# A GRU gate stage by one level of Strassen's product, with PSUM split in two pools

## The chip, the cores and the metric

The kernel runs on one core of a Trainium2 chip. The metric is the device time of one execution in microseconds; lower is better. TensorE multiplies matrices into PSUM (eight banks of 128 x 512 fp32), VectorE (DVE), ScalarE (ACT) and GpSimd (POOL) work elementwise, and DMA queues (issued from SyncE, SP, and from GpSimd) move data between HBM and SBUF. All numbers are fp32. In the profile an fp32 matmul appears as two MATMUL records, each with its weight load (PEld).

## The reference, cut to what matters

The input x holds 128 graphs of 128 nodes with 256 features. Layer 0 is a normalisation and ReLU, then a gated graph network; layer 1 is five small graph convolutions over the first 25 nodes of each graph. The change is in the gates of layer 0 (h is the normalised input, d = 256):

```python
x_in = concatenate([x_conv, x_nmp], axis=-1)       # 512 features
gi = x_in @ w_ih.T + b_ih                          # 512 -> 768
gh = h @ w_hh.T + b_hh                             # 256 -> 768
r = sigmoid(gi_r + gh_r)
z = sigmoid(gi_z + gh_z)
nn_ = tanh(gi_n + r * gh_n)
out0 = (1.0 - z) * nn_ + z * h
x = x + out0
```

x_conv is a pair of one-dimensional convolutions (1 tap and 17 taps), x_nmp a dense message passing over the adjacency.

## The kernel before, in words

The 128 graphs are worked on in 32 groups q of four graphs (4 x 128 = 512 columns, features on the partitions as two chunks of 128). Each group goes through these programs, which are Python generators:

- stage_a(q), eight groups per batch: load x (tile xa), normalise it, transpose it to hT (stored to HBM as hTd), first convolution (pc), Fourier transform of its nodes (pf) into X.
- stage_b(bat), four batches: the 17-tap convolution as products per frequency (pa, pb), with weights wf loaded from HBM and summed on GpSimd (lines 474, 475) and the results y combined on VectorE (lines 503 to 505) and stored to HBM as yd.
- stage_n(q): the messages (pse, pm, pd, pt, px) into xm.
- stage_c(q): the inverse transform (pi, line 638) and its ReLU give xc; then the gates (line 656); then the output.
- prepare(blk) and block(blk): layer 1, eight blocks of 16 graphs, in the second half.

The order of instructions on every engine is fixed before the run. `Order.run` takes steps from two lanes: a step ends at a `yield cost, delay`, and the lane with the least cost done (divided by its weight) goes next. Each engine then works through its own queue strictly in that order, and waits at semaphores where it needs another engine. The groups' lane runs stage_n and stage_c with two programs in flight; the other lane first holds stage_a and stage_b, then layer 1. Stage_c of the next group may start as soon as the last gate of the group before it is issued (G_DONE), and its output waits for the group before (C_DONE).

In stage_c the inverse transform makes, for each feature half co, one PSUM tile of 128 x 512 with eight matmuls, which VectorE then reads (line 640, scale and add hT) and ScalarE finishes (line 642). A gate is one PSUM tile of 128 x 512: six weight chunks of 128 x 128 for r and z (two on hT, two on xm, two on xc), and for n four chunks on xm and xc in one tile (pn) and two on hT in another (pg). The order is, for each half dc: r, pg, n, z. ScalarE takes sigmoid and tanh out of PSUM or SBUF (lines 662, 676, 681), VectorE does two operations (lines 666, 675), GpSimd three operations of 128 x 512 (lines 684, 685, 687): d = hT - n, d = d z, go = d + n. Then po transposes go back and VectorE adds it to x (line 706).

PSUM is two pools of four banks: pacc (pa, pb, pw, pi, the gates, the large tiles of layer 1 and half of the pd tiles) and ptmp (all else).

Of the kernel before, what the change touches and what calls it, by code (L numbers as in the profile page):

```python
# [9 lines left out]
FP = mybir.dt.float32  # L10
# [7 lines left out]
HID = 512  # L18
# [189 lines left out]
def kernel(ctx: ExitStack, tc: tile.TileContext, x, adj, consts, vecs, w_se, conv1_w,  # L208
# [8 lines left out]
    pacc = ctx.enter_context(tc.tile_pool(name="pacc", bufs=4, space=PSUM))  # L217
# [94 lines left out]

    def fold_embedding():

        nc.vector.memset(wse9, 0.0)
        for role in range(3):
            nc.vector.tensor_copy(wse9[:, :, 3 * role:3 * role + 3], wse[:, :, :3])
        pbs = ptmp.tile([P, 512], FP, tag="tmp", name="pbs")
        nc.tensor.matmul(pbs[:, :1], c("sel"), v("b_se"), start=True, stop=True)
        bse = cp.tile([P, 1], FP, name="bse")  # L320
        nc.vector.tensor_copy(bse, pbs[:, :1])
        nc.vector.scalar_tensor_tensor(embb, emb[:, 4:8], bse, emb[:, 8:12],
                                       op0=ALU.mult, op1=ALU.add)
        yield 1.5, 0.0
# [15 lines left out]
    def load_xa(q):  # L340
        LOADED.add(q)
        XA[q] = ab.tile([P, 4, D], FP, tag="xa", name=f"xa{q}", bufs=3)
        load_x(XA[q], q)

    def stage_a(q):
# [3 lines left out]
        for n in range(q, min(q + 3, NQ)):  # L349
            if n not in LOADED:  # L350
                load_xa(n)
# [6 lines left out]
        hT = ab.tile([P, 2, 512], FP, tag="hTa", name=f"hTa{q}")  # L358
# [7 lines left out]
        yield 0.9, 1.5  # L366
        nc.gpsimd.dma_start(out=hTd[q], in_=hT)
        h1 = ab.tile([P, GB, D], FP, tag="h1", name=f"h1{q}")
# [32 lines left out]
    def tap_weights():  # L401
# [23 lines left out]
        for n in range(4):  # L425
            for m in range(8):
                if m % 4 == 0:
                    ws = tw.tile([P, 2, 8, D], FP, tag="ws", name=f"ws{n}_{m}")
                pws = [pacc.tile([P, 2, D], FP, tag="acc", name=f"pw{n}_{m}_{h}")
# [16 lines left out]
        LATE["wih"] = weight(wg, w_ih, [P, 4, 3 * D], "(k p) o -> p k o", "wih", nc.sync)  # L446
        LATE["whh"] = weight(wg, w_hh, [P, 2, 3 * D], "(k p) o -> p k o", "whh", nc.sync)
# [6 lines left out]
    def stage_b(bat):  # L454
# [31 lines left out]
        for f in range(NF + 1):  # L486
# [5 lines left out]
            pa = pacc.tile([P, 2, D], FP, tag="acc", name=f"pa{bat}_{f}")  # L492
            for s in range(2):
                product(pa[:, s], lambda k: X[:, k, 2 * f + s], f, s)
            if f == 0:
                nc.vector.tensor_copy(y, pa)
            else:
                pac = xf.tile([P, 2, D], FP, tag="pac", name=f"pac{bat}_{f}", bufs=2)
                nc.scalar.activation(pac, pa, AF.Copy)  # L499
                pb = pacc.tile([P, D], FP, tag="acc", name=f"pb{bat}_{f}")  # L500
                xs = XS.pop(f)
                product(pb, lambda k: xs[:, k], f, 2)
                nc.vector.tensor_sub(y[:, 0], pac[:, 0], pac[:, 1])  # L503
                nc.vector.tensor_add(pac[:, 0], pac[:, 0], pac[:, 1])
                nc.vector.tensor_sub(y[:, 1], pb, pac[:, 0])
# [18 lines left out]
    def load_c2(q):  # L524
        yt = LATE["io"].tile([HB, 2 * GB, D], FP, tag="yt", name=f"yt{q}")
        x0 = q % BQ * 2 * GB
        nc.sync.dma_start(
            out=yt, in_=yd[q // BQ].rearrange("(x b) f c -> (b f) x c", b=NB // 2)
            [:, x0:x0 + 2 * GB])
        xt = LATE["io"].tile([P, 4, D], FP, tag="xt", name=f"xt{q}")  # L530
        load_x(xt, q)
        IN2[q] = yt, xt

    def neighbours(q, hT, ad, xm):
# [20 lines left out]
        for h in range(2):  # L555
            pm = ptmp.tile([P, 2, D], FP, tag="tmp", name=f"pm{q}_{h}")
            for i in range(2):
# [10 lines left out]
        pds = [(ptmp, pacc)[i % 2].tile([P, N], FP, tag=("tmp", "acc")[i % 2], name=f"pd{q}_{i}")  # L568
               for i in range(GB)]
        pt = ptmp.tile([P, GB, N], FP, tag="tmp", name=f"pt{q}")  # L570
        aT = LATE["fr"].tile([P, GB, N], FP, tag="aT", name=f"aT{q}")
        for j in range(GB):
            rows = slice(j * WIDE, (j + 1) * WIDE)
            nc.tensor.matmul(pds[j], lr[rows, 0], lr[rows, 1], start=True, stop=True)
        for j in range(GB):
            nc.tensor.transpose(pt[:, j], ad[:, j], ident)
        for j in range(GB):
            nc.scalar.activation(aT[:, j], pds[j], AF.Exp)
        nc.vector.tensor_mul(aT, aT, pt)
# [43 lines left out]
    def stage_c(q):  # L623
# [6 lines left out]
        if q not in IN2:  # L630
            load_c2(q)
            yield 0.0, 6.0
        yt, xt = IN2.pop(q)
        xc = LATE["fr"].tile([P, 2, 512], FP, tag="xc", name=f"xc{q}")
        for co in range(2):
            pc = pacc.tile([P, 512], FP, tag="acc", name=f"pi{q}_{co}")
            for a in range(2 * GB):
                nc.tensor.matmul(pc[:, a * 64:(a + 1) * 64], yt[:, a, co * P:(co + 1) * P],  # L638
                                 inv[:HB], start=True, stop=True)
            nc.vector.scalar_tensor_tensor(xc[:, co], pc, scl["bn2"][:, co:co + 1], hT[:, co],  # L640
                                           op0=ALU.mult, op1=ALU.add)
            nc.scalar.activation(xc[:, co], xc[:, co], AF.Relu, bias=sft["bn2"][:, co:co + 1])
            yield 1.75, 0.0

        xin = [(2, xm[:, 0]), (3, xm[:, 1]), (0, xc[:, 0]), (1, xc[:, 1])]
        wih, whh = LATE["wih"], LATE["whh"]
        go = LATE["fr"].tile([P, 2, 512], FP, tag="go", name=f"go{q}")

        def gate(ps, col, ih, hh):
            ops = []  # L650
            if hh:
                ops += [(whh[:, k, col:col + P], hT[:, k]) for k in range(2)]
            if ih:
                ops += [(wih[:, i, col:col + P], a) for i, a in xin]
            for i, (w, a) in enumerate(ops):
                nc.tensor.matmul(ps, w, a, start=(i == 0), stop=(i == len(ops) - 1))  # L656

        for dc in range(2):
            pr = pacc.tile([P, 512], FP, tag="acc", name=f"pr{q}_{dc}")
            gate(pr, dc * P, True, True)  # L660
            r = LATE["fr"].tile([P, 512], FP, tag="r", name=f"r{q}_{dc}")
            nc.scalar.activation(r, pr, AF.Sigmoid, bias=brz[:, dc:dc + 1])  # L662
            yield 5.2, 0.0
            ph = pacc.tile([P, 512], FP, tag="acc", name=f"pg{q}_{dc}")
            gate(ph, 2 * D + dc * P, False, True)
            nc.vector.scalar_tensor_tensor(r, ph, v("b_hh", 4 + dc), r, op0=ALU.add, op1=ALU.mult)
            yield 1.75, 0.0
            if not dc:
                while q and q - 1 not in C_DONE:
                    yield 0.0, 0.5  # L670
                if q + 1 < NQ and (q + 1) // BQ in B_DONE:
                    load_c2(q + 1)
            pn = pacc.tile([P, 512], FP, tag="acc", name=f"pn{q}_{dc}")
            gate(pn, 2 * D + dc * P, True, False)
            nc.vector.tensor_add(r, r, pn)  # L675
            nc.scalar.activation(r, r, AF.Tanh, bias=v("b_ih", 4 + dc))  # L676
            yield 3.45, 0.0
            pz = pacc.tile([P, 512], FP, tag="acc", name=f"pz{q}_{dc}")
            gate(pz, D + dc * P, True, True)
            z = LATE["fr"].tile([P, 512], FP, tag="z", name=f"z{q}_{dc}")  # L680
            nc.scalar.activation(z, pz, AF.Sigmoid, bias=brz[:, 2 + dc:3 + dc])  # L681

            d = LATE["fr"].tile([P, 512], FP, tag="d", name=f"d{q}_{dc}")
            nc.gpsimd.tensor_sub(d, hT[:, dc], r)  # L684
            nc.gpsimd.tensor_mul(d, d, z)  # L685
            pat = "p (j t n) -> p t j n"
            nc.gpsimd.tensor_add(go[:, dc].rearrange("p (t j n) -> p t j n", t=4, j=GB),
                                 d.rearrange(pat, j=GB, t=4), r.rearrange(pat, j=GB, t=4))
            if dc:
                G_DONE.add(q)  # L690
            yield 5.2, 5.5 * dc
# [3 lines left out]
        for h in range(2):  # L695
            po = ptmp.tile([P, 2, D], FP, tag="tmp", name=f"po{q}_{h}")
            for i in range(2):
                t = 2 * h + i
                for dc in range(2):
                    nc.tensor.transpose(po[:, i, dc * P:(dc + 1) * P],  # L700
                                        go[:, dc, t * P:(t + 1) * P], ident)
# [18 lines left out]
    def setup_1():  # L720
# [11 lines left out]
        S["w1"] = weight(pool, W1, [P, 5, 2, HID], "g (k p) o -> p g k o", "w1", nc.sync)  # L732
# [31 lines left out]
        yield 0.5, 0.0  # L764

# [89 lines left out]
    def block(blk):  # L855
# [3 lines left out]
        w1, w2, ac, r4 = S["w1"], S["w2"], S["ac"][blk % 2], S["r4"][blk % 2]  # L859
# [14 lines left out]
        def first(g):  # L874
            n, o = SIZES[g], OFFS[g]
            hh = hs[g] = pool.tile([P, 4, SB, n], FP, tag="hh0" if g == 0 else "hh",
                                   name=f"hh{blk}_{g}", bufs=1 if g == 0 else 2)
            for m in range(4):
                ph = pacc.tile([P, SB, n], FP, tag="acc", name=f"ph1{blk}_{g}_{m}")
                for k in range(2):  # L880
                    nc.tensor.matmul(ph, w1[:, g, k, m * P:(m + 1) * P],  # L881
# [3 lines left out]
        def second(g):  # L885
            n, o = SIZES[g], OFFS[g]
            for cc in range(2):
                pz = pacc.tile([P, SB, n], FP, tag="acc", name=f"pz1{blk}_{g}_{cc}")
# [5 lines left out]
        for g in range(NG + 1):  # L894
# [3 lines left out]
            if g:  # L898
                second(g - 1)
                yield 5.5 if g == 1 else 1.95, 0.0 if g < NG else 1.0  # L900

# [48 lines left out]
    order.run(begin, beside, until=begin)  # L950
    order.run(Lane([stage_b(0)]), beside)
# [50 lines left out]
```

## Time and profile before

| | |
|---|---|
| runs shown, us | 2342.34, 2342.02, 2337.05; median 2342.02 |
| the profiled execution, us | 2334.82 |
| its span, us | 2333.0 |
| mean granted TensorE clock | 0.98 |
| VectorE, us from 1400 to 1800 | 127.12 busy of 400 |
| TensorE, us from 1400 to 1800 | 394.78 busy of 400 |

A row of the groups reads: line, engine, operation, output<-input, shapes, count | busy us in total, mean ns of one | idle us of the engine just before them, and what ended it. A row of the timeline begins with its start in us from the span's start and its length in us; merged rows have a count. Ends of matmuls are modelled: of several matmuls in a row, the last one's end is drawn later than the pace of their starts.

### The profile page before, as it was taken

To read this page: it belongs to the slowest core of one execution; us is meant where nothing else is said; L and a number is where in the kernel's file an instruction comes from. 1 tells how busy PE (TensorE), PEld (TensorE's weight loads), DVE (VectorE), ACT (ScalarE), POOL (GpSimd) and SP (SyncE) were. 2 spreads that over 40 slices of the span, in tenths; PEclk is the share of its full clock that TensorE was granted. 3 is DMA by queue.
4 is the path that set the end of the run, shared out by engine and by line. 5 is a ranking of instruction groups with operands and counts; after the bars stand their busy time and mean duration, and the time that the engine had idled before them with its cause. 6 is when DMAs were issued, how large, how long until landed. Compare 5 with 4: busy or idle time off the path is not lost.

```text
span 2333.0 us, 27381 instructions
## 1 busy us (share of the span) xinstructions
PE 2234.0 (96%) x10284; PEld 1456.6 (62%) x10284; DVE 881.9 (38%) x1787; ACT 631.9 (27%) x1169; POOL 791.2 (34%) x977
## 2 busy tenths in 40 slices
PE   3979899999999999999999999999999999999997
PEld 2558766666667666666666656656566555665675
DVE  2546734334344334444343334223223222222242
ACT  1432222211123322233322222222322222213132
POOL 2215422355532255422255533223213222222230
PEclk7989999999999999999999999999999999999999
DMA  9777653445532343524245451121212211212000
GB/s 146 211 243 243 211 139 105 113 129 175 162 108 82 118 133 121 165 69 118 73 144 146 134 164 46 46 64 39 53 32 67 61 28 33 64 43 63 8 16 19
DMA packets 180714, 241.08 MB, mean 103 GB/s; under 512 B 20849, under 2 KB 151734, under 8 KB 179046
## 3 DMA queue, kind: packets, MB, share of 16 engines
q1 hardware_dynamic: 152070, 156.29, 24.3%
q0 software_dynamic: 27952, 82.54, 12.2%
q8 instruction: 82, 1.34, 0.2%
q10 hardware_dynamic: 560, 0.49, 0.1%
q14 instruction: 50, 0.41, 0.1%
HBM read 160.08 MB, written 79.17 MB: 103 GB/s over the span
## 4 chain that ended last, share of the span: by engine, by line
PE 88%; DMA 4%; DVE 3%; POOL 2%; issue 2%; ACT 1%; SPq 0%; POOLq 0%; DVEq 0%; ACTq 0%
PE pr L656 14%; PE pz L656 14%; PE pn L656 9%; PE pa L480 6%; PE pi L638 5%; PE pm L560 5%; PE pg L656 5%; PE pc L373 4%; PE ph L881 4%; PE pz L890 4%; PE pf L386 3%; PE pb L480 3%; PE px L587 2%; DMA hT<-hTd 1%; PE ph L362 1%
## 5 line engine op out<-in xcount | busy, mean ns | idle before, releaser
L684 POOL TENSOR_TENSOR d<-hT,r 128x512 f32<-128x512 f32 x64 | 81.3, 1270 | 406.1 <-ACT r L676 288.7
L685 POOL TENSOR_TENSOR d<-d,z 128x512 f32<-128x512 f32 x64 | 81.5, 1273 | 318.7 <-ACT z L681 283.6
L480 PE MATMUL pa<-wf,X 128*128 128x256 f32 x768 | 182.1, 380 | 0.0
L480 PEld LDWEIGHTS pa<-wf,X 128*128 128x128 f32 x768 | 144.3, 190 | 43.0 <-issue 26.0
L503 DVE TENSOR_TENSOR y<-pac 128x256 f32<-128x256 f32 x92 | 73.6, 800 | 254.8 <-ACT pac L499 251.2
L656 PE MATMUL pr<-hT,whh 128*128 128x512 f32 x256 | 128.7, 627 | 3.5 <-DVE yz L892 3.5
L278 POOL TENSOR_TENSOR rs<-rs,cst 128x4 f32<-128x4 f32 x40 | 41.2, 1031 | 248.1 <-DVE rs L277 237.9
L560 PE MATMUL pm<-wmsg,hT 128*128 128x256 f32 x512 | 125.3, 390 | 0.0
L475 POOL TENSOR_TENSOR wf<-wf 128x512 f32<-128x512 f32 x92 | 124.8, 1357 | 1.2 <-DMA wf<-wfd 1.2
L373 PE MATMUL pc<-c1w,hTa 128*128 128x256 f32 x512 | 125.1, 394 | 0.0
L638 PEld LDWEIGHTS pi<-cst,yt 96*128 96x128 f32 x1024 | 121.3, 194 | 2.5 <-issue 1.2
L638 PE MATMUL pi<-cst,yt 96*128 96x64 f32 x1024 | 122.0, 275 | 0.3 <-ACT hh L883 0.3
L656 PE MATMUL pg<-hT,whh 128*128 128x512 f32 x256 | 122.0, 599 | 0.0
L656 PE MATMUL pz<-hT,whh 128*128 128x512 f32 x256 | 121.6, 597 | 0.0
L373 PEld LDWEIGHTS pc<-c1w,hTa 128*128 128x128 f32 x512 | 98.5, 197 | 35.1 <-issue 15.3
L656 PE MATMUL pz<-xc,wih 128*128 128x512 f32 x256 | 120.3, 592 | 0.0
L656 PE MATMUL pn<-xc,wih 128*128 128x512 f32 x256 | 120.3, 592 | 0.0
L656 PE MATMUL pr<-xc,wih 128*128 128x512 f32 x256 | 120.3, 592 | 0.0
L676 ACT ACTIVATE r<-r,vec 128x512 f32<-128x512 f32 x64 | 46.2, 722 | 269.2 <-DVE r L675 269.2
L881 PE MATMUL ph<-yz,w 128*128 128x96 f32 (+3 forms) x640 | 109.1, 323 | 4.7 <-DVE yz L892 2.0
L662 ACT ACTIVATE r<-pr,brz 128x512 f32<-128x512 f32 x64 | 44.0, 687 | 249.1 <-PE pr L656 234.6
L560 PEld LDWEIGHTS pm<-wmsg,hT 128*128 128x128 f32 x512 | 97.3, 194 | 21.3 <-issue 8.4
(165 smaller groups left out, 3918.8 us busy)
## 6 DMA issues: line engine op xcount, KB each, us to landing
wf<-wfd SPq DMA_DIRECT2D x192, 256.0 KB, 3.1
yd<-y POOLq DMA_DIRECT2D x96, 256.0 KB, 2.4
yt<-yd SPq DMA_DIRECT2D x32, 768.0 KB, 7.5
hT<-hTd SPq DMA_DIRECT2D x40, 512.0 KB, 4.0
xa<-in_x SPq DMA_DIRECT2D x128, 128.0 KB, 3.0
hTd<-hTa POOLq DMA_DIRECT2D x32, 512.0 KB, 4.3
xt<-in_x SPq DMA_DIRECT2D x128, 128.0 KB, 2.8
wfd<-ws POOLq DMA_DIRECT2D x32, 384.0 KB, 9.9
```

The costliest lines, as they stand in the source:

```text
L373: nc.tensor.matmul(pc[:, i], hT[:, k, (2 * h + i) * N:(2 * h + i + 1) * N], c1w[:, k], start=(k == 0), stop=(k == 1))
L386: nc.tensor.matmul(pf[:, i, :F * NB], h1[:, 2 * h + i, k * P:(k + 1) * P], fwd, start=True, stop=True)
L475: nc.gpsimd.tensor_tensor(WF[f][:, :, 2], WF[f][:, :, 0], WF[f][:, :, 1], ALU.add)
L480: nc.tensor.matmul(ps, xk(k), WF[f][:, k, s], start=(k == 0), stop=(k == 1))
L503: nc.vector.tensor_sub(y[:, 0], pac[:, 0], pac[:, 1])
L560: nc.tensor.matmul(pm[:, i], hT[:, k, j * N:(j + 1) * N], wmsg[:, k], start=(k == 0), stop=(k == 1))
L638: nc.tensor.matmul(pc[:, a * 64:(a + 1) * 64], yt[:, a, co * P:(co + 1) * P], inv[:HB], start=True, stop=True)
L656: nc.tensor.matmul(ps, w, a, start=(i == 0), stop=(i == len(ops) - 1))
L684: nc.gpsimd.tensor_sub(d, hT[:, dc], r)
L685: nc.gpsimd.tensor_mul(d, d, z)
L881: nc.tensor.matmul(ph, w1[:, g, k, m * P:(m + 1) * P], yz[:, k, :, o:o + n], start=(k == 0), stop=(k == 1))
L890: nc.tensor.matmul(pz, w2[:, g, m, cc * P:(cc + 1) * P], hs[g][:, m], start=(m == 0), stop=(m == 3))
```

## The change

The gates r and z (on hT, xm and xc) and the part of n that comes from xm and xc are no longer computed as six (or four) weight chunks per 512 columns. The two weight chunks of an operand (k = 0, 1), the two output halves (for r and z: r and z themselves; for n: its two halves dc) and the two halves of the columns are taken as 2 x 2 block matrices, and multiplied by one level of Strassen's product in Winograd's form: seven products of blocks instead of eight. Three products take blocks of the operand itself, four take sums of blocks, which VectorE makes for each operand (tiles th, tm, tc). The weight sums are made once on GpSimd (fold_gates). A product accumulates its operands (three for r and z, two for n) in a PSUM tile of 128 x 2 x 256 (r, z) or 128 x 256 (n), and VectorE adds the products up into r, z and, for n, straight into r.

The rest of the diff follows from the room this needs. PSUM's pool of the gates (pgat, four banks) serves the gates alone, and everything else shares ptmp's four. The inverse transform makes one tile per half of the columns h, with the two feature halves co in it, and VectorE and ScalarE treat each co by itself. yt is loaded per h, xt later and in one buffer, W1 in pieces of one graph convolution, the gate weights in thirteen loads. Stage A has one buffer for hT and for h1 and two for xa. The four pd tiles hold the transposed adjacency too, and VectorE multiplies them one by one.

```diff
+    def fold_gates():
+        for w in (LATE["wrz"], LATE["wn"]):
+            nc.gpsimd.tensor_sub(w[:, 6], w[:, 0], w[:, 4])
+            nc.gpsimd.tensor_add(w[:, 4], w[:, 4], w[:, 3])
+            nc.gpsimd.tensor_sub(w[:, 5], w[:, 4], w[:, 0])
+            nc.gpsimd.tensor_sub(w[:, 2], w[:, 1], w[:, 5])
+            nc.gpsimd.tensor_scalar(w[:, 3], w[:, 3], -1.0, None, op0=ALU.mult)
...
+        def sums(name, x, eng):
+            t = fr.tile([P, 4, D], FP, tag=name, name=f"{name}{q}")
+            eng.tensor_sub(t[:, 0], x[:, 0, D:], x[:, 0, :D])
+            eng.tensor_sub(t[:, 1], x[:, 1, D:], t[:, 0])
+            eng.tensor_sub(t[:, 2], x[:, 1, D:], x[:, 0, D:])
+            eng.tensor_sub(t[:, 3], t[:, 1], x[:, 1, :D])
+            return t
+        th = sums("th", hT, nc.vector)
+        tm = sums("tm", xm, nc.vector)
+        xc = fr.tile([P, 2, 512], FP, tag="xc", name=f"xc{q}")
+        for h in range(2):
+            yt = IN2.pop((q, h))
+            s = slice(h * D, (h + 1) * D)
+            pc = ptmp.tile([P, 2, D], FP, tag="tmp", name=f"pi{q}_{h}")
+            for co in range(2):
+                for a in range(GB):
+                    nc.tensor.matmul(pc[:, co, a * 64:(a + 1) * 64], yt[:, a, co * P:(co + 1) * P],
+                                     inv[:HB], start=True, stop=True)
+                nc.vector.scalar_tensor_tensor(xc[:, co, s], pc[:, co], scl["bn2"][:, co:co + 1],
+                                               hT[:, co, s], op0=ALU.mult, op1=ALU.add)
+                nc.scalar.activation(xc[:, co, s], xc[:, co, s], AF.Relu,
+                                     bias=sft["bn2"][:, co:co + 1])
+            load_yt(q + 1, h)
             yield 1.75, 0.0
...
+        tcs = sums("tc", xc, nc.vector)
...
+        def product(w, i, xs):
+            n = w.shape[3] // P
+            ps = pgat.tile([P, n, D], FP, tag="gat", name=f"p{n}{q}_{i}")
+            for m in range(n):
+                for j, (k, x, t) in enumerate(xs):
+                    nc.tensor.matmul(ps[:, m], w[:, i, k, m * P:(m + 1) * P], factor(i, x, t),
+                                     start=(j == 0), stop=(j == len(xs) - 1))
+            return ps
...
+        xs = [(0, hT, th), (2, xm, tm), (1, xc, tcs)]
+        nc.scalar.activation(r1, product(wrz, 0, xs), AF.Copy)
+        yield 2.6, 0.0
+        nc.vector.tensor_tensor(u2, r1, product(wrz, 5, xs), ALU.add)
+        yield 2.6, 0.0
...
+        xs = [(1, xm, tm), (0, xc, tcs)]
+        nc.scalar.activation(v1, product(wn, 0, xs), AF.Copy)
+        yield 0.87, 0.2
...
+        nc.vector.tensor_tensor(r12, r12, product(wn, 2, xs), ALU.add)
+        for dc in (1, 0):
+            nc.scalar.activation(r[:, dc], r[:, dc], AF.Tanh, bias=v("b_ih", 4 + dc))
+            d = fr.tile([P, 512], FP, tag=f"u{2 + dc}", name=f"d{q}_{dc}")
+            nc.gpsimd.tensor_sub(d, hT[:, dc], r[:, dc])
+            nc.gpsimd.tensor_mul(d, d, z[:, dc])
...
+        G_DONE.add(q)
+        yield 0.87, 9.0
```

## The prediction

> **What bounds the kernel now.** I read the page's busy shares first, then the chain that ended last, then the chain's pieces.
>
> ```profile
> span 2333.0 us, 27381 instructions
> PE 2234.0 (96%) x10284; PEld 1456.6 (62%) x10284; DVE 881.9 (38%) x1787; ACT 631.9 (27%) x1169; POOL 791.2 (34%) x977
> PE 88%; DMA 4%; DVE 3%; POOL 2%; issue 2%; ACT 1%; SPq 0%; POOLq 0%; DVEq 0%; ACTq 0%
> 339.86 5.15 PE pz L656 x12
> ```
>
> TensorE is the bound: 96% busy, 88% of the chain. Twelve 512-column records take 5.15 us, 0.429 us each. The timeline gives the 256-column pace, and it shows something else:
>
> ```profile
> 503.64 1.89 PE L480 MATMUL pa<-wf,X 128*128 128x256 f32 x8
> 505.37 1.03 PE L480 MATMUL pb<-wf,xs 128*128 128x256 f32 x4
> 506.01 1.26 POOL L687 TENSOR_TENSOR go<-d,r 128x512 f32<-128x512 f32 x1
> 506.25 1.29 DVE L503 TENSOR_TENSOR y<-pac 128x256 f32<-128x256 f32 x1 [6.09 <-ACT pac L499]
> 507.23 0.91 POOL L474 TENSOR_TENSOR xs<-X 128x256 f32<-128x256 f32 x1
> 507.58 0.83 DVE L504 TENSOR_TENSOR pac<-pac 128x256 f32<-128x256 f32 x1
> 508.10 1.45 POOL L475 TENSOR_TENSOR wf<-wf 128x512 f32<-128x512 f32 x1
> 508.52 0.42 DVE L505 TENSOR_TENSOR y<-pb,pac 128x256 f32<-128x256 f32 x1
> ```
>
> From 503.64 to 505.37 eight records ran: 0.216 us each, half of 0.429, so a half-wide matmul wastes nothing. In the lower rows VectorE and GpSimd take turns. L503 (both inputs in SBUF) ends at 507.54, 0.27 us after GpSimd's L687 ends at 507.27; L504 at 508.41, 0.27 after L474's 508.14. L505, one input of which is in PSUM, runs its 0.42 straight through L475. The groups say the same:
>
> ```profile
> L504 DVE TENSOR_TENSOR pac<-pac 128x256 f32<-128x256 f32 x92 | 75.9, 825 | 3.2
> L505 DVE TENSOR_TENSOR y<-pb,pac 128x256 f32<-128x256 f32 x92 | 39.0, 424 | 9.6
> ```
>
> Last, what a pause costs TensorE afterwards:
>
> ```profile
> 1385.87 1.08 PE L540 MATMUL pse<-hT,wse 128*32 128x128 f32 x16 [5.03 <-DMA hT<-hTd]
> 1386.88 3.51 PE L656 MATMUL pr<-hT,whh 128*128 128x512 f32 x4
> 1390.22 1.88 PE L656 MATMUL pr<-xnmp,wih 128*128 128x512 f32 x4
> ```
>
> After 5.03 us idle, four records take 1390.22 - 1386.88 = 3.34 us instead of 1.72: half clock, 1.6 us lost.
>
> **What it removes.** Per group of four graphs, 32 products of 512 columns (64 records) become 7x2x3 + 7x1x2 = 56 products of 256 columns (112 records): 64 x 0.429 = 27.5 us against 112 x 0.216 = 24.2. That is 3.3 us a group, 32 groups: **-104 us**, all on the path.
>
> **What it adds on the path.** In the changed program's order every group's last product (p_2 of wn) is followed on TensorE by the next group's pi_0, in 30 of 31 cases with both pi tiles and nothing between. VectorE stands in this order: the add of p_2 into r; four differences of hT (th); four of xm (tm); then the pi adds (L640's operation, now 128x256). New, too, is a wait: pi was two tiles, each written whole by eight matmuls and then read. Now a tile has two halves, four matmuls each, and the second half's first matmul waits for VectorE's read of the first half: in all 64 tiles the fifth matmul waits on VectorE. So TensorE does 4 x 2 records (16 took 1.90 us, so 0.9 us) and stops until VectorE has done one add, eight differences and one pi add. Queued behind it is the whole kernel's TensorE order.
>
> The length, from p_2's end: 0.2 us for the modelled end of p_2 and the hop; add, 0.42 (L505); eight differences; pi add, 0.45 (between L505's 0.42 and half of L640's 748 ns plus its fixed part); hop 0.06; less the 0.9 of cover. All eight differences read two SBUF inputs, as L504 does. With GpSimd idle each is 0.424 us: 3.4 together. But at this place GpSimd begins its six 128x512 operations on d and z (L684, L685, L687: 1.27 each), as tanh of the n gate releases them. A difference that meets them ends once per GpSimd operation, each 1.27 to 1.45 (the 1.45 is L475 with L504 in front): 8 differences are 3.4 us with none met, 9.5 with six met. The first half of d is often done early, as other lanes' matmuls stand between p_3 and p_2 (p_3 releases dc 1, p_2 dc 0), so I take four met: 4 x 1.4 + 4 x 0.42 = 7.3. Stop: 0.2 + 0.42 + 7.3 + 0.45 + 0.06 - 0.9 = **7.5 us** (3.6 to 9.7). The second pi tile stops again for one pi add, 0.16 + 0.04 + 0.45 + 0.06 = 0.7. After a stop over 5 us the clock row adds 1.6 (0 if short, 3 if the half clock holds for its full stretch). One boundary: 7.5 + 0.7 + 1.6 = 9.8 us; 31 of them: **+304 us** (133 to 415).
>
> The Trainium skill, "SBUF — State Buffer", section "Who interferes with whom", says that a VectorE instruction with two SBUF inputs contends with a GpSimd instruction that reads SBUF, and the second to issue blocks fully until the first is done. Read strictly, a met difference would end 0.42 after the GpSimd operation, not 0.27 as the rows have it: 4 x 0.15 x 31 = 19 us more on the sum. I keep the rows' figure.
>
> The same skill, "TensorE: Matmul & The Clock Gate", section "HAM oscillation — how this bites in real kernels", warns of idle gaps above some 3.4 us, after which the array runs at half clock for a window. By it each boundary would lose some 1.7 us, 53 in all, against my 50; it speaks against this change, which makes 31 such gaps where the trace of before has few.
>
> **What it adds beside the path.** VectorE, per group: 12 differences (four on xc, after pi, covered by p_0's 12 records and p_5's first four, 3.5 us, against 2.0 for add, relu and two differences); seven 128x512 adds at 0.69 (L675's 687 ns); eleven 128x256 adds at 0.42, less two old 0.69. Some 442 us (645 if every two-SBUF operation takes 0.82) on 882: about 1,400 of 2,500, no bound. ScalarE gets two copies (0.6, 0.35) and shorter sigmoids. GpSimd folds the gate weights once: ten operations of 768 or 256 columns, some 13 us by L475's rate, near the end of the first Fourier stage (49 of 90 us busy there); cover gone, 13 us. Weights in 13 loads, W1 in 40 of 0.5 MB: the DMA engines are one or two tenths busy in the second half, nothing. xt with one buffer waits for the previous group's output on SP's queue, as the two-buffer load one group ahead did: nothing.
>
> All else now shares four PSUM buffers, eight before, and stage A has one hT and h1 buffer and two of xa. In the steady part the covers are three tiles (2.6 to 5 us) against releases of 0.6 to 2.7 us: nothing. From 50 to 290 us, where the kernel already stalls, a hTd store (4.3 us to landing) can show per group, eight of them: 0 to 50 us, I take 15. A gain of up to 20 us is possible too, as stops soak up TensorE's small waits of after 1400 us.
>
> **Sum.** The profiled execution took 2334.82 us (span 2333.0), 7 under the median of the three runs, 2342.02. -104 + 304 + 15 = +215: 2550.
>
> **Rivals.** (a) GpSimd rarely meets the differences: stop 3.6 + 0.7, clock 0.5: 31 x 4.8 = 149, and 2335 - 104 + 149 + 15 = 2395. For it: L504 was free in part of its cases. Against: the order puts GpSimd's six operations at that very place. (b) Faster: the wait at pi's second half costs under 104 / 31 = 3.4 us a boundary, because the differences are short or done before p_2 ends; at nothing, 2335 - 104 + 15 = 2246. Against: the add of p_2 stands ahead of them in VectorE's order, and eight at 0.42 alone are 3.4. (c) Worse: all six met, VectorE also late from its n adds by 1 to 2 us, half clock for 3 us: 31 x 15 = 465, + 50: 2746. (d) The product saves nothing because weight loads bind: excluded, 256-column records ran at 0.216 with a load of 0.19 beside each.
>
> **How the numbers follow.** Forecast 0.72, its own range 2455 to 2660; (a) 0.15; (b) 0.06; (c) 0.07; of (a) and (b) 0.01 each end within 0.3%. The range 2400 to 2680 leaves out (b), half of (a)'s lower part and most of (c). About 0.3% is what a measurement here can tell from no change. Faster 0.05, same 0.02, slower 0.93.
>
> **What would show it.** Right: TensorE's records near 112 x 0.216 a group for the gates; a TensorE idle row at pi (line 675) released by VectorE's xc, some 7 us, 31 times; granted clock below 0.95 in the steady part; the differences' mean between 0.8 and 1.3 us. Wrong if pi's idle is under 100 us in total, or if stalls sit in ptmp tiles of other lanes or in the first 300 us.

## The result and the profile after

The changed kernel takes **2753.12 us** (median of four runs, 2749.96 to 2758.25), the kernel before 2341.72 us (median of four, 2337.05 to 2342.34): ratio 1.1764, 95% interval 1.1737 to 1.1791, 411 us slower. The direction was forecast, the size was not: 2550 us was named and the range ended at 2680. The time is that of rival (c), 2746 us, which had been given a chance of 0.07.

The page of the changed kernel, in the order in which the page before was read: span, busy shares, granted clock in 40 slices, the chain that ended last, and the costliest group.

```profile
span 2748.2 us, 32012 instructions
PE 2305.5 (84%) x11820; PEld 1884.4 (69%) x11820; DVE 1404.3 (51%) x2843; ACT 711.4 (26%) x1423; POOL 818.2 (30%) x987
PEclk7989888898878999888989888898989989889899
PE 76%; DVE 17%; DMA 3%; POOL 2%; issue 2%; ACT 1%; SPq 0%; DVEq 0%; POOLq 0%; ACTq 0%
...
L675 PE MATMUL pi<-cst,yt 96*128 96x64 f32 x1024 | 211.9, 385 | 309.2 <-DVE xc L677 309.2
```

TensorE falls from 96% to 84% busy, and VectorE carries 17% of the chain instead of 3%, though it is only half busy. The group row tells where: TensorE stood 309.2 us idle just before pi's matmuls, all of it ended by VectorE's xc. The same two rows of the kernel before, the clock and pi's matmuls (there line 638):

```profile
PEclk7989999999999999999999999999999999999999
L638 PE MATMUL pi<-cst,yt 96*128 96x64 f32 x1024 | 122.0, 275 | 0.3 <-ACT hh L883 0.3
```

The matmuls of pi were busy for 122.0 us before the change and take 211.9 us now, and the clock row shows eights where it had nines: this work at half speed is the second loss.

One boundary between two groups, in the timeline of the changed kernel (start, length, engine, line; in brackets the idle time before it and what ended it):

```profile
1320.82 1.00 PE L675 MATMUL pi<-cst,yt 96*128 96x64 f32 x8
1321.02 0.42 DVE L771 TENSOR_TENSOR r<-r,p 128x256 f32<-128x256 f32 x1 [1.06 <-PE p L697]
1321.36 0.42 DVE L660 TENSOR_TENSOR th<-hT 128x256 f32<-128x256 f32 x1
1321.54 1.36 POOL L776 TENSOR_TENSOR d<-hT,r 128x512 f32<-128x512 f32 x1 [7.12 <-ACT r L773]
1321.81 1.38 DVE L661 TENSOR_TENSOR th<-hT,th 128x256 f32<-128x256 f32 x1
1322.98 1.32 POOL L777 TENSOR_TENSOR d<-d,z 128x512 f32<-128x512 f32 x1
1323.11 1.48 DVE L662 TENSOR_TENSOR th<-hT 128x256 f32<-128x256 f32 x1
...
1330.12 0.41 DVE L663 TENSOR_TENSOR tm<-tm,xnmp 128x256 f32<-128x256 f32 x1
1330.45 0.47 DVE L677 SCALAR_TENSOR_TENSOR xc<-pi,s_bn,hT 128x256 f32<-128x256 f32 x1
...
1330.98 3.67 PE L675 MATMUL pi<-cst,yt 96*128 96x64 f32 x16 [9.16 <-DVE xc L677]
1335.23 1.97 PE L675 MATMUL pi<-cst,yt 96*128 96x64 f32 x8 [0.58 <-DVE xc L677]
1337.00 3.58 PE L387 MATMUL pc<-c1w,hTa 128*128 128x256 f32 x8
```

TensorE issues pi's first eight records and stops. VectorE adds p_2, makes eight differences and only then reads pi. Six differences lie beside a GpSimd operation (lines 776 to 779, twice three, without a gap) and take 1.4 to 1.5 us each, the other two 0.42. After 9.16 us TensorE goes on, at half speed: 16 pi records took 1.90 us in the kernel before and take 3.67 here, then another 0.58 us of waiting, and eight records of pc take 3.58 us, against 1.89 at 1345.60. The windows of the trace around this boundary give the clock (columns: window, its length, then each engine's busy time with its instructions, granted clock, DMA share, GB/s):

```profile
1326.70:1330.98 4.28, 0.00 (x0) 0.00 (x0) 4.19 (x5) 0.02 (x1) 3.62 (x4) 0.50 0.00 0
1330.98:1340.40 9.42, 8.84 (x32) 8.02 (x33) 1.45 (x3) 2.01 (x4) 0.00 (x0) 0.50 0.49 156
1340.40:1350.00 9.60, 9.60 (x50) 8.50 (x49) 5.18 (x14) 1.86 (x3) 0.00 (x0) 1.00 0.48 122
```

The half clock began inside the stop and lasted 9.42 us after it, of which TensorE was busy for 8.84. So this boundary costs the stop, and some 4.4 us more (half of 8.84).

**Where the 415 us of span went** (2748.2 against 2333.0). I took the pitch between the starts of consecutive matmuls, its usual value for each kind of matmul, and the excess over it; up to a doubling inside a stretch of half clock is counted as clock, the rest as waiting. This is an estimate from the trace, good to some 10 us.

| us | before | after | difference |
|---|---|---|---|
| gates, 64 x 0.429 against 112 x 0.216 a group | 878 | 774 | -104 |
| waiting at pi | 0 | 320 | +320 |
| other waiting of TensorE | 222 | 277 | +55 |
| lost to half clock | 25 | 169 | +144 |

The sum is +415. (The profile's own row for the wait at pi is 309.2; the pitches have it as 320.)

### The profile page after: what moved, and what is told of

It is laid out like the page before. It is cut to its first block, busy times and chain, and to the rows that moved or that the text cites. A ratio compares the mean times of both kernels' runs of the same rounds, so it can differ in the third digit from the quotient of the medians.

```text
span 2748.2 us, 32012 instructions
## 1 busy us (share of the span) xinstructions
PE 2305.5 (84%) x11820; PEld 1884.4 (69%) x11820; DVE 1404.3 (51%) x2843; ACT 711.4 (26%) x1423; POOL 818.2 (30%) x987
## 4 chain that ended last, share of the span: by engine, by line
PE 76%; DVE 17%; DMA 3%; POOL 2%; issue 2%; ACT 1%; SPq 0%; DVEq 0%; POOLq 0%; ACTq 0%
PE p L697 29%; PE pi L675 6%; PE pa L503 6%; PE pg L742 4%; PE pc L387 4%; PE pm L582 4%; PE pz L990 3%; PE ph L981 3%; PE pf L400 3%; PE pb L503 2%; PE px L607 2%; DVE th L663 2%; DVE tm L660 1%; DVE th L662 1%; DVE tm L661 1%
## 5 line engine op out<-in xcount | busy, mean ns | idle before, releaser
L675 PE MATMUL pi<-cst,yt 96*128 96x64 f32 x1024 | 211.9, 385 | 309.2 <-DVE xc L677 309.2
L675 PEld LDWEIGHTS pi<-cst,yt 96*128 96x128 f32 x1024 | 201.7, 294 | 321.7 <-DVE xc L677 319.6
L679 ACT ACTIVATE xc<-xc,t_bn 128x256 f32<-128x256 f32 x128 | 65.0, 508 | 421.5 <-DVE xc L677 421.5
L697 PE MATMUL p<-th,wrz 128*128 128x256 f32 x512 | 154.0, 382 | 0.0
L697 PE MATMUL p<-tc,wrz 128*128 128x256 f32 x512 | 152.3, 379 | 0.0
L697 PE MATMUL p<-tm,wrz 128*128 128x256 f32 x512 | 152.3, 379 | 0.0
L697 PE MATMUL p<-hT,wrz 128*128 128x256 f32 x384 | 141.1, 454 | 0.0
L497 POOL TENSOR_TENSOR xs<-X 128x256 f32<-128x256 f32 x92 | 68.9, 749 | 210.6 <-PE pb L503 189.6
L697 PE MATMUL p<-xc,wrz 128*128 128x256 f32 x384 | 130.1, 424 | 0.0
L742 PE MATMUL pg<-hT,whn 128*128 128x512 f32 x256 | 123.8, 613 | 0.0
```

Source lines behind the costliest of these rows:

```text
L497: nc.gpsimd.tensor_tensor(XS[f], X[:, :, 2 * f], X[:, :, 2 * f + 1], ALU.add)
L675: nc.tensor.matmul(pc[:, co, a * 64:(a + 1) * 64], yt[:, a, co * P:(co + 1) * P], inv[:HB], start=True, stop=True)
L697: nc.tensor.matmul(ps[:, m], w[:, i, k, m * P:(m + 1) * P], factor(i, x, t), start=(j == 0), stop=(j == len(xs) - 1))
L742: nc.tensor.matmul(pg, whn[:, k, dc * P:(dc + 1) * P], hT[:, k], start=(k == 0), stop=(k == 1))
```

## The experiments

In the table, "half clock" is the loss by the estimate above. Every ratio is to the kernel before, measured beside the kernel of its row. e1, e2, e4 and e5 have two runs each, the others four to ten.

| kernel | us, median | ratio, 95% interval | TensorE's main wait at the boundary, us | half clock, us |
|---|---|---|---|---|
| before | 2341.72 | | none | 25 |
| changed | 2753.12 | 1.1764 (1.1737 to 1.1791) | pi 309.2 | 169 |
| e1, pi in two whole tiles | 2572.4 | 1.0996 (1.0939 to 1.1054) | first product 190.1 | 111 |
| e2, differences behind pi | 2472.05 | 1.0568 (1.0506 to 1.0629) | pi 62.9 | 103 |
| e3, both, raw products first | 2332.23 | 0.9957 (0.9937 to 0.9977) | first product 4.7 | 44 |
| e4, stop filled with matmuls | 2693.67 | 1.1515 (1.1454 to 1.1576) | pi 70.8 | 107 |
| e5, GpSimd's blending away | 2573.14 | 1.0988 (1.0936 to 1.104) | pi 139.5 | 162 |
| e6, before with PSUM split | 2396.95 | 1.0243 (1.0204 to 1.0282) | none at pi | 41 |
| e7, before with shared pi tiles | 2465.98 | 1.0522 (1.0484 to 1.0559) | pi 63.2 | 83 |
| e8, e3 with banks handed back | 2264.14 | 0.9666 (0.9649 to 0.9683) | first product 3.9 | 29 |
| e9, e7 with a fill in each tile | 2432.39 | 1.0392 (1.0378 to 1.0406) | pi 22.9 | 43 |
| e10, e8 with the fold spread | 2258.35 | 0.9641 (0.9621 to 0.9662) | first product 4.0 | 26 |

### e1: pi in two whole tiles

```diff
-        for h in range(2):
-            pc = ptmp.tile([P, 2, D], ...)
-            for co in range(2):
-                for a in range(GB):
-                    (matmul into half co of the tile; add and relu of that half)
+        for co in range(2):
+            pc = ptmp.tile([P, 512], ...)
+            for a in range(2 * GB):
+                (matmul); (add and relu of the whole tile)
```

> The changed kernel with the inverse transform in one PSUM tile per feature half again (written whole, then read), so that no matmul waits inside a pi tile. The eight differences of hT and xm still stand ahead of the pi reads on VectorE. Theory (the differences ahead in VectorE's order are the cause, the shared tile only sets where it shows): the idle row at pi goes and comes back at the first product's xc operand, 7 us a boundary instead of 9.6: some 220 us of idle, time 2630 to 2690. Rival (the wait inside the tile is the cause): the idle goes altogether, with the half clock: 2300 to 2380.

2572.4 us, between the two forecasts. The wait at pi is gone; in the waits of e1 it stands at the next tile (engine, tile and line, releaser: us in total, times, longest):

```profile
PE p L696 <- ACT xc L677: 190.1, 31, 11.1
```

31 times 6.1 us: pi's matmuls no longer wait inside a tile, but the first product needs xc, and xc still stands behind the differences in VectorE's queue. Taking away only the shared tile removes 119 us of the 309 (309.2 - 190.1); taking away only the place of the differences (e2, below) removes 246 at pi, so the two shares overlap. e1 also shows what a stop costs when full-sized products follow it and no further wait: its half clock is 86 us above the kernel before's (111 - 25), 2.8 us for each of 31 stops, though part of it lies elsewhere (see e6).

### e2 and e3: the differences behind pi, and the raw products first

e2 leaves pi as changed and moves two lines:

```diff
-        th = sums("th", hT, nc.vector)
-        tm = sums("tm", xm, nc.vector)
         xc = fr.tile([P, 2, 512], FP, tag="xc", name=f"xc{q}")
         (the loop over pi)
+        th = sums("th", hT, nc.vector)
+        tm = sums("tm", xm, nc.vector)
         tcs = sums("tc", xc, nc.vector)
```

> The changed kernel with the differences of hT and xm issued after the pi reads, ahead of those of xc; the tile shared by both feature halves stays. Theory: idle at pi falls from 309 us to about 40 (64 waits of 0.6), and the wait moves to the first product that takes sums (twelve differences, two or three of them met by GpSimd, against 3.5 us of cover): 3 to 5 us a boundary, time 2520 to 2600. Rival (the wait inside the tile is the cause): pi's idle stays near 300 and the time near 2750.

2472.05 us, better than the 2520 to 2600 expected. In the waits of e2:

```profile
PE pi L673 <- DVE xc L675: 62.9, 64, 10.0
...
PE p L697 <- DVE tc L661: 11.2, 13, 1.2
```

What is left at pi is 64 waits, most of them of 0.58 us for the add alone; a few are longer, up to 10.0. The differences cost less too: VectorE's busy time falls from 1404.3 to 1274.8 us, because fewer of them meet GpSimd at the later place (the eight of a group take 4.5 us together instead of 8.5). The products that need them hardly wait.

e3 adds e1's tiles, and computes the three products that take no sums (0, 1, 2) ahead of 5, 4, 6 and 3:

```diff
-        nc.scalar.activation(r1, product(wrz, 0, xs), AF.Copy)
-        nc.vector.tensor_tensor(u2, r1, product(wrz, 5, xs), ALU.add)
+        nc.scalar.activation(u2, product(wrz, 0, xs), AF.Copy)
+        th, tm, tcs = (the twelve differences)
+        nc.vector.tensor_tensor(r1, u2, product(wrz, 1, xs), ALU.add)
+        nc.scalar.activation(r2, product(wrz, 2, xs), AF.Copy)
+        nc.vector.tensor_tensor(u2, u2, product(wrz, 5, xs), ALU.add)
```

> Both edits together, and the three products that take no sums first (0, 1, 2, then 5, 4, 6, 3), so that 7.7 us of matmuls cover the twelve differences; it costs one more copy on ScalarE and one more add on VectorE. Theory: boundary idle under 1 us, half clock rare, so 2748 - 309 - 144 + 15 = 2310, range 2260 to 2360: the saving of the seven products shows, faster than before or equal. Rival (VectorE's whole load, 51% busy, or four PSUM banks for all else hold TensorE back anywhere): 2450 or more.

2332.23 us, as forecast, and 421 us below the changed kernel with the same products and differences. From the groups of e3, the wait that is left ahead of the first product's xc:

```profile
L693 PE MATMUL p<-xc,wrz 128*128 128x256 f32 x384 | 117.2, 387 | 4.7 <-ACT xc L675 4.7
```

VectorE is still 1320.7 us busy there: its work was never too much, only in the wrong place.

### e4: matmuls in the stop

```diff
+                if q and (h, co) == (0, 0):
+                    fill = pgat.tile([P, 512], FP, tag="gat", name=f"fill{q}")
+                    for _ in range(9):
+                        nc.tensor.matmul(fill, LATE["whn"][:, 0, :P], hT[:, 0], start=True, stop=True)
```

> The changed kernel with nine 128x512 matmuls (18 records, 7.7 us) into an unread tile put between the two halves of the first pi tile of each group but the first: they do nothing but keep TensorE at work while it would wait, and the output is the same. Theory that half clock after each stop costs 4 us a boundary: the idle at pi falls by 31 x 7.7 to about 70, that is no gain by itself, but half clock goes and the time falls by 100 to 150, to 2600 to 2650. Rival, the prediction's 1.6 us: 2690 to 2710. If the clock is of no effect: 2748.

2693.67 us, 59 less than the changed kernel. That lies inside the rival's 2690 to 2710, by which the stop costs the prediction's 1.6 us of clock, and is not the 100 or more that a half clock brought on by the long stop alone would have given back. By the table the half clock falls by 62 us (169 to 107), 2.0 a boundary: this much goes with the long stop. The other 82 us above the kernel before stay. In e4's timeline the 18 records of the fill run at full pace, and half clock follows all the same:

```profile
1302.51 7.94 PE L684 MATMUL fill<-hT,whn 128*128 128x512 f32 x18
1311.84 2.36 PE L675 MATMUL pi<-cst,yt 96*128 96x64 f32 x16 [1.39 <-DVE xc L677]
1314.78 1.97 PE L675 MATMUL pi<-cst,yt 96*128 96x64 f32 x8 [0.58 <-DVE xc L677]
1316.54 3.73 PE L387 MATMUL pc<-c1w,hTa 128*128 128x256 f32 x8
```

With waits of only 1.39 and 0.58 us around pi's small matmuls, eight records of pc still take 3.73 us.

### e5: GpSimd taken off the boundary

```diff
-            d = fr.tile([P, 512], FP, tag=f"u{2 + dc}", name=f"d{q}_{dc}")
-            nc.gpsimd.tensor_sub(d, hT[:, dc], r[:, dc])
-            nc.gpsimd.tensor_mul(d, d, z[:, dc])
-            nc.gpsimd.tensor_add(z[:, dc]..., d..., r[:, dc]...)
+            nc.scalar.activation(z[:, dc]..., r[:, dc]..., AF.Copy)
```

> The changed kernel without GpSimd's six operations on d and z: ScalarE copies the n gate into z's place instead, so the blending (1 - z) n + z h is left out. Theory: with GpSimd idle each difference takes 0.42 us, the stop at pi falls from 9 to 3.6 us plus 0.6 for the second tile, 130 us of idle instead of 309, and most of the half clock goes with it: 2470 to 2530. Rival (the length of the queue alone, GpSimd not involved): differences stay near 1.1 us, time 2730 to 2750.

2573.14 us; this kernel leaves out the blending (1 - z) n + z h and serves for its time alone. One line of the groups of each kernel, a th difference of the changed kernel and then, in the second fence, of e5 (busy us, mean ns):

```profile
L663 DVE TENSOR_TENSOR th<-th,hT 128x256 f32<-128x256 f32 x32 | 45.2, 1414 | 0.0
```

```profile
L663 DVE TENSOR_TENSOR th<-th,hT 128x256 f32<-128x256 f32 x32 | 13.4, 418 | 0.0
```

With GpSimd away every difference takes 0.42 us, and pi's wait falls from 309.2 to 139.5 us (130 had been expected): 170 us of the wait was VectorE taking turns with GpSimd. The time fell by 180 us and not by the 223 or more expected, because the half clock's share stayed, 162 against 169 us. By the timelines, the first wait of a group's pi is 3.6 us on average over the 31 boundaries here and 9.1 in the changed kernel: between these two lengths the clock cost does not change.

### e6: PSUM split, nothing else

The kernel before, with its gates in one pool of four banks, all else in the other, and the pd tiles as in the change.

```diff
-    pacc = ctx.enter_context(tc.tile_pool(name="pacc", bufs=4, space=PSUM))
+    pgat = ctx.enter_context(tc.tile_pool(name="pgat", bufs=4, space=PSUM))
...
-            pa = pacc.tile([P, 2, D], FP, tag="acc", name=f"pa{bat}_{f}")
+            pa = ptmp.tile([P, 2, D], FP, tag="tmp", name=f"pa{bat}_{f}")
```

> The kernel before with only PSUM split as in the change: four banks for the gates alone, four for everything else, and the message stage's tiles as in the change. Gates and inverse transform as before. Theory that sharing four banks costs what the changed trace shows beside pi (pd, pb, pa, pc, pw, some 55 us more waiting than before, mostly before 400 us): 2370 to 2400. Rival, the prediction's view that the cover hides it: 2335 to 2350.

2396.95 us, 55 more than the kernel before. Its waits hold rows of pd and pa that the kernel before does not have among its larger ones:

```profile
PE pd L572 <- DVE y L505: 13.6, 9, 2.3
PE pd L572 <- DVE yz L890: 6.3, 4, 4.1
PE pa L480 <- DVE aT L577: 4.6, 7, 2.4
```

Many small waits in all phases, most under 2.5 us and the longest of these rows 4.1. By the pitches they make 43 us, 38 of them at pd, and bring 16 us of half clock (41 against 25).

### e7 and e9: shared pi tiles in the kernel before, and a fill

e7 gives the kernel before the changed kernel's pi loop (two halves in one tile), and nothing of the products or differences. e9 adds to e7 one 128x512 matmul between the halves of each tile:

```diff
+                if not co:
+                    fill = pacc.tile([P, 512], FP, tag="acc", name=f"fill{q}_{h}")
+                    nc.tensor.matmul(fill, LATE["whh"][:, 0, :P], hT[:, 0], start=True, stop=True)
```

> The kernel before with only the inverse transform changed: a tile per column half with both feature halves in it, so each tile's fifth matmul waits for VectorE's read of its first half. No differences, gates as before. Theory: VectorE has nothing else queued, so each of the 64 waits costs 0.6 to 0.7 us: 2375 to 2395. Rival (the wait itself is dear, 9 us): over 2600. If it is hidden: 2342.

> The kernel before with the inverse transform in column halves (2466), and one 128x512 matmul (0.86 us) into an unread tile between the halves of each pi tile, so that TensorE works through its wait. It adds 64 x 0.86 = 55 us of work and covers 64 waits of 0.6 to 1.0 us. Theory that the halves' 126 us are some 63 us of waiting and some 57 us of half clock, which the short waits bring on: waits near 0 to 10, half clock as in the kernel before, 2342 + 55 + 10 = 2390 to 2420. Rival (the half clock comes from pi's small matmuls, not from the waits): 2460 or more.

e7 missed by far, 2465.98 us where 2395 had been the upper end. The waits at pi in e7:

```profile
PE pi L640 <- DVE xc L643: 63.2, 64, 4.0
```

The wait itself is somewhat longer than expected, 1 us on average instead of 0.6 to 0.7; another 58 us are half clock (83 against 25), in 34 stretches against 12, most of them of 3.4 or 6.8 us. e9 gives TensorE 55 us more to do (128 records at 0.429) and is 34 us faster than e7, 12 us above the upper end of its forecast; its waits at pi are 22.9 us in 19 places, its half clock 43 us. The kernel before has the same small matmuls without the waits and loses 25 us. So the half clock here follows from repeated waits of about 1 us among small matmuls too, not only from long stops. But the rival named for e9 has a part in it. In the 3.4 us before eight of e7's 27 half-clock stretches from 400 us on, TensorE waited only 0.6 to 0.7 us and spent 1.8 to 2.6 us on pi's matmuls; and in e1 four stretches begin behind 3.4 us of pi's matmuls with no wait at all. One of them, in e1's timeline, where the two records of p take 1.17 us instead of 0.59:

```profile
1302.43 3.74 PE L673 MATMUL pi<-cst,yt 96*128 96x64 f32 x32
...
1305.96 1.17 PE L696 MATMUL p<-hT,wrz 128*128 128x256 f32 x2
```

How much of the loss is the waits' and how much the small matmuls', these runs do not divide: e9's fill both takes away the wait and puts a large matmul among the small ones.

With this the 144 us of the changed kernel can be divided, as an estimate: 16 us come with the four banks (e6), 58 with the short waits in pi's tiles (e7), and the 70 us left, 2.3 a boundary, with the long stops. e1, which has the long stops and the four banks but no wait inside a tile, has the same 70 (111 - 25 - 16), the four stretches among them. That the shares simply add is assumed. The clock's records in all these traces change in steps of 3.4 us. The Trainium skill, "TensorE: Matmul & The Clock Gate", section "A second HAM failure mode: psum-queue depth-cycling", speaks of a kernel that idles only briefly, but often, between groups of matmuls, and whose clock oscillates; e7, with its 34 stretches, agrees. What share of idle time within a step brings the half clock on was not measured.

### e8 and e10: the banks handed back, and the fold spread

e8 is e3, with the tap weights' tiles (pw), the first batch's pa and pb, and two of the four pd tiles in the gates' pool. The first two are done before the gates begin.

```diff
-                pws = [ptmp.tile([P, 2, D], FP, tag="tmp", ...
+                pws = [pgat.tile([P, 2, D], FP, tag="gat", ...
...
+        pool, tag = (ptmp, "tmp") if bat else (pgat, "gat")
...
-        pds = [ptmp.tile([P, 2, N], FP, tag="tmp", name=f"pd{q}_{j}") for j in range(GB)]
+        pds = [(ptmp, pgat)[j % 2].tile([P, 2, N], FP, ...) for j in range(GB)]
```

> The kernel with the three sum-free products first and pi whole (2332), and beside it the gates' four banks lent out while no gate runs: the tap weights and the first batch's Fourier products take them, and two of the four message tiles pd. Theory that the shared four banks cost what the split alone cost (57 us, of which pd some 40): 2270 to 2310, faster than the kernel before by 1.5 to 3%. Rival (the rest of the waiting comes from VectorE's load, and banks only show it): 2320 to 2340.

2264.14 us, 6 below the lower end of the forecast, 68 less than e3 and 3.3% faster than the kernel before.

e10 puts a step's end behind each of fold_gates' ten operations, so that they are spread over the last frequencies of the first batch.

```diff
             nc.gpsimd.tensor_sub(w[:, 6], w[:, 0], w[:, 4])
+            yield 0.0, 4.0
             nc.gpsimd.tensor_add(w[:, 4], w[:, 4], w[:, 3])
+            yield 0.0, 4.0
```

> The kernel with the banks handed back (2264 us), with the ten GpSimd operations that fold the gate weights put between the last steps of the first batch's tap convolution, instead of all ten at once ahead of its last three frequencies. In the changed kernel and in the one with the banks handed back, TensorE waits once 13.1 us at pb for a GpSimd weight sum that is queued behind them. Theory (the cover of that step was gone, 13 us): the single wait of 13.1 us falls below 4 us and nothing else moves, 2250 to 2257 us. Rival (the ten operations only move the wait: VectorE's and GpSimd's later work, or the first folded product at 340 us, waits in its place): a row of 8 us or more between 290 and 350 us at another tile, 2260 to 2268 us.

2258.35 us; its interval overlaps with that of e8, so a gain is not shown. The wait of 13.1 us at pb has fallen to 2.7 in two places, and the rival's other wait is there, in the timeline of e10 (13.21 us at ph, where e8 has 5.23):

```profile
312.75 0.85 POOL L326 TENSOR_SCALAR wn<-wn 128x256 f32<-128x256 f32 x1
313.57 1.04 POOL L278 TENSOR_TENSOR rs<-rs,cst 128x4 f32<-128x4 f32 x1
314.64 1.38 DVE L283 TENSOR_SCALAR xa<-xa,mv,rs 128x256 f32<-128x256 f32 x4 [5.63 <-POOL rs L278]
315.11 2.30 PE L378 MATMUL ph<-cst,xa 128*128 128x128 f32 x8 [13.21 <-DVE xa L283]
```

The rest of the fold now stands on GpSimd's queue ahead of the next group's normalisation (rs), which VectorE and then TensorE wait for. The ten operations have to go somewhere else, not only apart.

## Why the prediction was wrong, by its own steps

- **Gates, -104 us: right.** The timeline of after has two 256-column records every 0.43 us, as in the sum. e8 confirms the total: its span is 70 us below the kernel before's (2262.7 against 2333.0), with 31 us more waiting and 3.5 us more half clock by the pitches; 70 + 31 + 3.5 = 105.
- **The stop at pi: mechanism right, size short, 254 us forecast (31 x 8.2), 309.2 measured.** Of these, 3.9 us belong to the first group, which has no group ahead of it; the 31 boundaries have 9.85 each. The step that failed is "so I take four met". In the trace three to seven of the eight differences are met at a boundary (over 0.9 us long), 5.3 on average, and the eight take 8.7 us together, against 7.3 in the forecast. The reason given for four, that the first half of d is often done early, holds seldom: only at eight of the 31 boundaries are three or four met, and at the one shown above all six GpSimd operations run in one row behind the last add. That is 1.4 us a boundary, of the 1.65 by which 9.85 exceeds 8.2; the rest was not resolved.
- **Half clock, 1.6 us a boundary, 50 us: wrong, the largest miss.** It was 144 us; all put on the boundaries, 4.6 each, beyond the forecast's upper bound of 3. The forecast took the price from one place of the kernel before where, after the stop, full-sized matmuls followed without a gap, and gave the short waits inside pi's tiles no clock cost at all. By the estimate under e9, the long stops cost 2.3 us each, the short waits 58 us and the four banks 16. e4, which fills the stop, gives back 2.0 us a boundary: the price of the stop was short by a little, and what was left out is the larger part. The length of the stop makes no difference between 3.6 and 9.1 us (e5).
- **The buffers of everything else, 15 us: wrong.** The steady part was put at nothing, and e6, where only PSUM is divided, costs 55 us. The forecast compared covers of 2.6 to 5 us with releases of 0.6 to 2.7 us tile by tile and took each release as prompt; in e6's rows pd and pa wait for VectorE's y, yz and aT, a little at a time. In the changed kernel the other waiting is 55 us more, of which pd has 28 and fold_gates 13. The hTd store, for which the 15 us stood, shows in one wait of TensorE, 8.9 us at pc.
- **fold_gates, "cover gone, 13 us": that case came true, though the sum had left it out.** The waits of after have it:

```profile
PE pb L503 <- POOL wf L498: 13.1, 1, 13.1
```

- **Beside the path:** VectorE was forecast at about 1,400 us and was busy 1404.3 us; it was no bound, as e3 shows. (The operations listed there add up to some 420 us, not 442.)
- **The rivals:** (a) and (b) are refuted by the row at pi. (c) hit the time: 15 us a boundary, and it was 10.3 of stop (the pitches' 320 over 31) and 4.6 of clock, 14.9; its + 50 for the rest stands against 55. Its reason holds in part: five to six differences met, and a half clock beyond even its 3 us. Its "VectorE also late", 1 to 2 us, has no row of its own here and stands in its sum where the clock's missing 1.6 would be: that it met the time so closely is in part luck.
- **The signs named beforehand:** pi's idle row released by xc was there, at 9.1 us a stop instead of 7; the mean of the eight differences is 1.07 us, inside the 0.8 to 1.3 (0.72 to 1.41 line by line); the clock is 0.884 over the run, and 0.87 to 0.90 in the steady part, below 0.95. Of the two signs against the forecast, the stalls of other lanes' tiles came true beside it (e6), though smaller.

So the forecast had the right place and failed on three sizes, all in one direction: + 66 at pi (320 against 254), + 94 of half clock, + 40 of other waits, 200 us in all, which is the 203 by which the measured median exceeds 2550.

## What to carry to other kernels

Saving a fraction of the matmuls paid here only once the sums that it needs stood behind the reads that TensorE was waiting for: the same products and differences gave 2753 us as they were, 2332 with another order and whole pi tiles (e3), and 2264 with the banks handed back as well (e8), against 2342 without them. Two halves of one PSUM tile, written and read by turns, made TensorE wait for the reader in every tile (64 waits in e7). Price a recurring stop by what runs after it as well as by its length: a stop of some 6 us with full-sized matmuls behind it cost 2.8 us of half clock at most (e1), one with small matmuls and further short waits behind it 4.6.

## What the hardware showed that was not expected

Waits of 1 us on average around matmuls of 64 columns, twice in each group and none over 4.0 us, cost the kernel before nearly as much in half clock (58 us in e7) as in waiting (63 us), and a 0.86 us matmul of no use put in their place made it 34 us faster. Stops of 3.6 us on average and of 9.1 were followed by nearly the same loss (162 and 169 us over the run). A VectorE difference with two SBUF inputs beside a busy GpSimd goes one for one with GpSimd's operations, at 1.4 to 1.5 us instead of 0.42, as long as GpSimd has a next one ready.
